# A block's last addition left to the next block or to the end, and a residual put ahead of a gate's step

## The chip, the cores and the metric

The kernel runs on one core of a Trainium2 chip. The metric is the time of one execution on the device in microseconds (us), as the median of a few runs. Beside it stands one profiled execution, which has its own time; the profile's span, from the first to the last instruction, is a little shorter than that time.

The engines: TensorE (PE; its weight loads are PEld), VectorE (DVE), ScalarE (ACT), GpSimd (POOL) and SyncE (SP, which here only issues DMAs). A "q" behind a name (POOLq) is the engine's sequencer: semaphore waits, branches, issuing.

## The reference, cut to what matters

```python
B, S, D = 4, 1024, 256            # T = B*S = 4096 tokens, 8 experts, hidden size 1024
x = x + ga * attention_like_scan(layernorm(x) * (1 + ca) + sa)      # y @ W_out, gated; "x1"
h = layernorm(x) * (1 + cb) + sb
scores = softmax(h @ Wg + bg);  top 2 experts per token, weights normed to 1
for e in range(8):
    y = gelu(h @ W1[e] + b1[e]) @ W2[e] + b2[e]
    output = output + y * combine_w[..., e]      # zero for experts that were not chosen
return x + gb * output
```

`ga`, `ca`, `sa`, `gb`, `cb` and `sb` come from a small product of the conditioning vector, one row per batch. All is float32.

## The kernel before, in words

**First part.** The 4096 tokens are cut into 8 chunks of 512. A chunk's projections, scan and output product run on all engines, interleaved with the second layernorm, the gate and the top-2 choice of earlier chunks. `o_pe` computes a chunk's output product into two PSUM tiles (`pya`), `o_resid` adds each to the residual `x` on VectorE (line 479) and stores the sum to `out`. `f_gate` computes the gate's logits on TensorE (line 540) and adds the bias on VectorE (line 547). The two PSUM slots of `pya` are those of `pye` below: the pool `ps_y` has two.

**Second part.** Each expert has a list of its tokens in DRAM. The lists are cut into blocks of 256 places; a block is two halves of 128. A table computed on the chip says which expert and which places block `j` has. Whole blocks come first, then blocks in which only the first half has tokens, then nothing. Up to 39 blocks are possible; 28 are surely whole, 32 surely exist. For block `j`:

- `fetch(j)`: `fetch_rows(j + 2)` loads the list entries (`ent`: a token's number and its weight; SyncE, line 788; four buffers in turn from block 8 on) and gathers the tokens' rows of `hx` into `hb` (GpSimd, line 801, one gather for each half, three buffers); `fetch_weights(j + 1)` loads `W1`, `b1`, `W2` and `b2` of its expert (SyncE, lines 819 to 822, two buffers, 2.1 MB per block).
- `b_up(j)`: the product with `W1` (line 859), gelu on ScalarE (line 868).
- `b_turn(j + 1)`: TensorE turns the next block's rows (line 843), VectorE copies them out of PSUM (`xT`, line 845).
- `b_down(j)`: for each half the product with `W2` (line 877, PSUM `pye`), then on VectorE the bias (line 885) and the weight and gate (line 886) into `yb`, which has four buffers, then on GpSimd one indirect DMA that adds the 128 rows to `out` (line 891). The DMA takes its row numbers from `ent`. Two blocks can share a token, so a block's additions wait until those of the block before have landed; the two halves of one block don't wait for each other.

**Order.** Every engine's order is the order in which the program is written (`manual_schedule`), so an engine that waits holds everything behind it. Waits are put in where an instruction reads or overwrites what another one, or a DMA, has yet to finish.

**Branches.** From block 28 on, `work_either` (line 1059) chooses between a whole and a half block; from block 32 on, `rest(j)` (line 1090) first asks whether block `j` exists, and the next block stands inside it. In each branch that skips DMAs of GpSimd, the queue of GpSimd increments the semaphores that they would have raised, in one instruction (INC_SWDGE_SEM in the profile), after waiting for what was raised before. In the branch for "no more blocks" this covers all eight such semaphores, and the increment waits for every DMA of GpSimd that is still under way. Behind the branches stands the end of the program: SyncE waits for all DMAs, each engine drains, and a barrier closes it (line 1125). With this input 36 blocks run: 0 to 30 are whole and 31 to 35 are half.

Of the kernel before, what the change touches and what calls it, by code (L numbers as in the profile page):

```python
# [9 lines left out]
F32 = mybir.dt.float32  # L10
I32 = mybir.dt.int32
AF = mybir.ActivationFunctionType
ALU = mybir.AluOpType
# [6 lines left out]
def tile_adaln_block(  # L20
# [32 lines left out]
    nc = tc.nc  # L53
    P = 128
    B, S, D = x.shape
    H = W_out.shape[0]
    E, _, F = W1.shape
    T = B * S
# [9 lines left out]
    HK = TK // P  # L68
# [16 lines left out]
    out_rows = out.rearrange("b s d -> (b s) d")  # L85

    const = ctx.enter_context(tc.tile_pool(name="const", bufs=1))
    apool = ctx.enter_context(tc.tile_pool(name="attn", bufs=1))
    deep = ctx.enter_context(tc.tile_pool(name="deep", bufs=2))
    work = ctx.enter_context(tc.tile_pool(name="work", bufs=3))  # L90
    small = ctx.enter_context(tc.tile_pool(name="small", bufs=2))
    xpool = ctx.enter_context(tc.tile_pool(name="blocks", bufs=2))
# [365 lines left out]
    def o_pe(c_):  # L458
        z, wo = X[c_]["z"], WO[c_ // NB]
        X[c_]["py"] = []  # L460
        for q in range(TPB // 2):
            py = ps_y.tile([P, 2, D], F32, tag="y", name=f"pya_{c_}_{q}")
            X[c_]["py"].append(py)
            for t in range(2):
                for hc in range(HC):
                    nc.tensor.matmul(  # L466
                        py[:, t, :],
                        lhsT=z[hc][:, ts(2 * q + t, P)],
                        rhs=wo[:, hc, :],
                        start=(hc == 0),  # L470
                        stop=(hc == HC - 1),
                    )

    def o_resid(c_):
        xb = X[c_]["x"]
        b, i = divmod(c_, NB)
        for q in range(TPB // 2):
            at = ds(2 * q, 2)
            nc.vector.tensor_add(xb[:, at, :], xb[:, at, :], X[c_]["py"][q])  # L479

        x1_stores.append(
            nc.sync.dma_start(
                out=out[b].rearrange("(n p) d -> p n d", p=P)[:, ts(i, TPB), :], in_=xb
            )
        )

    def f_stats(c_):
        X[c_]["stats"] = stats(X[c_]["x"], f"f{c_}")
# [43 lines left out]
    def f_gate(c_):  # L532
        b, i = divmod(c_, NB)
        if i == 0:
            R[b] = {"p": small.tile(sh, F32, tag="p", name=f"p_{b}")}
        hT = X[c_]["hT2"]
        pl = ps_tr.tile([P, TPB, E], F32, tag="tr", name=f"pl_{c_}")
        for n in range(TPB):
            for k in range(KC):
                nc.tensor.matmul(  # L540
                    pl[:, n, :],
                    lhsT=hT[:, k, ts(n, P)],
                    rhs=wg_sb[:, k, :],
                    start=(k == 0),
                    stop=(k == KC - 1),
                )
        nc.vector.tensor_add(
            R[b]["p"][:, ts(i, TPB), :], pl, bg_sb.unsqueeze(1).broadcast_to((P, TPB, E))
        )
# [221 lines left out]
    def seen(j: int):  # L771
        return EARLY_B * S if j < NE else T
# [18 lines left out]
    def fetch_rows(j: int):  # L791

        if j >= NJ:
            return
        if j >= NE:
            fetch_entries(j)
        hb = []
        for t in range(HK):
            g = turns(xpool, 3, [P, 2 * D], F32, f"hb{t}", j)
            BK[j]["gathers"].append(  # L800
                nc.gpsimd.indirect_dma_start(  # L801
                    out=g, out_offset=None, in_=hx[: seen(j), :],
                    in_offset=IndirectOffsetOnAxis(ap=BK[j]["ent"][:, t, 0:1], axis=0),
                    bounds_check=seen(j) - 1, oob_is_err=False,
                )
            )
            hb.append(g)
        BK[j]["hb"] = hb

    def fetch_weights(j: int):  # L810
        if j >= NJ:
            return
        wpool = pools["w"]
        e = entry(j, 0, E - 1)
        w1 = turns(wpool, 2, [P, KC, F], F32, "w1", j)
        w2 = turns(wpool, 2, [P, FC, D], F32, "w2", j)
        bb = turns(wpool, 2, [P, FC], F32, "bb", j)
        b2b = turns(wpool, 2, [P, D], F32, "b2b", j)
        nc.sync.dma_start(out=w1, in_=W1r[e])
        nc.sync.dma_start(out=bb, in_=b1d[e])  # L820
        nc.sync.dma_start(out=w2, in_=W2r[e])
        nc.sync.dma_start(out=b2b, in_=b2[ds(e, 1), :].broadcast_to((P, D)))
        BK.setdefault(j, {}).update(w1=w1, w2=w2, bb=bb, b2b=b2b)

    def fetch(j: int):

        fetch_rows(j + 2)
        fetch_weights(j + 1)
# [9 lines left out]
    def b_turn(j: int):  # L838
        hb = BK[j]["hb"]
        pt = ps_tr.tile([P, KC, TK], F32, tag="tr", name=f"ptx_{j}")  # L840
        for k in range(KC):
            for t in range(HK):
                nc.tensor.transpose(pt[:, k, ts(t, P)], hb[t][:, ts(k, P)], ident)  # L843
        xT = turns(xpool, 2, [P, KC, TK], F32, "xT", j)
        nc.vector.tensor_copy(xT, pt)  # L845
        BK[j]["xT"] = xT

    def b_up(j: int, half: bool = False):
        w1, bb, xT = (BK[j][n] for n in ("w1", "bb", "xT"))
        g = xpool.tile([P, FC, TK], F32, tag="g", name=f"g_{j}_{half}", bufs=1)  # L850
        BK[j]["g"] = g
        n = P if half else TK
        at_once = TB // n
        for f2 in range(FC // at_once):
            ph = ps_mm.tile([P, at_once, n], F32, tag="mm", name=f"ph_{j}_{f2}_{half}")
            for u in range(at_once):
                fc = at_once * f2 + u
                for k in range(KC):
                    nc.tensor.matmul(  # L859
                        ph[:, u, :],  # L860
                        lhsT=w1[:, k, ts(fc, P)],
                        rhs=xT[:, k, :n],
                        start=(k == 0),
                        stop=(k == KC - 1),
                    )
            for u in range(at_once):
                fc = at_once * f2 + u
                nc.scalar.activation(  # L868
                    g[:, fc, :n], ph[:, u, :], AF.Gelu_apprx_tanh, bias=bb[:, fc : fc + 1]
                )  # L870

    def b_down(j: int, half: bool = False, mid=None):
        g, w2, b2b, ent, hb = (BK[j][n] for n in ("g", "w2", "b2b", "ent", "hb"))
        for t in range(1 if half else HK):
            py = ps_y.tile([P, D], F32, tag="y", name=f"pye_{j}_{t}_{half}")
            for fc in range(FC):
                nc.tensor.matmul(  # L877
                    py,
                    lhsT=g[:, fc, ts(t, P)],
                    rhs=w2[:, fc, :],  # L880
                    start=(fc == 0),
                    stop=(fc == FC - 1),
                )
            yb = xpool.tile([P, D], F32, tag="yb", name=f"yb_{j}_{t}_{half}", bufs=4)
            nc.vector.tensor_add(yb, py, b2b)  # L885
            nc.vector.scalar_tensor_tensor(  # L886
                yb, yb, ent[:, t, 1:2].bitcast(F32), hb[t][:, D:], ALU.mult, ALU.mult
            )
            if t > 0:
                nc.gpsimd.memset(between, 0.0)  # L890
            ins = nc.gpsimd.indirect_dma_start(  # L891
                out=out_rows[: seen(j)],
                out_offset=IndirectOffsetOnAxis(ap=ent[:, t, 0:1], axis=0),
                in_=yb, in_offset=None, bounds_check=seen(j) - 1, oob_is_err=False,
                compute_op=ALU.add,
            )
            for other in BK[j]["acc"]:
                tc.declare_no_dep(ins.ins, other.ins, reason="a block's tokens are distinct")
            BK[j]["acc"].append(ins)
            if t == 0 and mid is not None:  # L900
                mid()
# [114 lines left out]
    last = NCH - 1  # L1016
# [4 lines left out]
    r_rank_pe(B - 2)  # L1021
    b_turn(1)
    o_pe(last)
    f_gate(last - 1)
    o_resid(last)
    f_stats(last)
    r_place(B - 2)
    drain(4)
# [20 lines left out]
    b_down(2)  # L1049
    tab["l"], ends_at = late_table()  # L1050

    def work(j: int, half: bool = False):
        b_up(j, half)
        if j + 1 < NJ:
            b_turn(j + 1)
        b_down(j, half)

    def work_either(j: int):
        with tc.If(n_whole > j) as whole:  # L1059
            work(j)  # L1060
        with whole.Else():
            work(j, True)


    sure_whole = (2 * T - E * P) // TK
    sure = 2 * T // TK
# [17 lines left out]
    )  # L1084
    for j in range(sure_whole, sure):
        fetch(j)
        work_either(j)

    def rest(j: int):
        with tc.If(n_blocks > j):  # L1090
            fetch(j)
            work_either(j)
            if j + 1 < NJ:
                rest(j + 1)

    rest(sure)
    order.close()


# [30 lines left out]
```

## Time and profile before

| | |
|---|---|
| median of 3 runs | 828.38 us (826.85 to 828.54) |
| profiled execution: its time, its span | 828.35 us, 826.6 us |
| TensorE busy | 802.2 us, 97% of the span |
| VectorE, ScalarE, GpSimd busy | 348.9, 250.7, 300.4 us |
| additions to `out` (line 891) | 62 of whole blocks, 5 of half blocks, 1.6 us each on GpSimd |
| one whole block, from addition to addition | 14.25 us |
| granted TensorE clock | 0.992 |

A row of the timeline has its start, its length, engine, line, operation and tiles, and in brackets how long the engine had been idle and what ended that. A row of a view of one line has the engine, the operation and the count, then the shortest, median and longest duration in ns, then the first and the last start in us. A row of the waits has who waited, for whom, the sum in us, the times and the longest. "DMA to landing" runs from the start of the DMA's row to the last of its data.

### The profile page before, as it was taken

To read this page: it belongs to the slowest core of one execution; us is meant where nothing else is said; L and a number is where in the kernel's file an instruction comes from. 1 tells how busy PE (TensorE), PEld (TensorE's weight loads), DVE (VectorE), ACT (ScalarE), POOL (GpSimd) and SP (SyncE) were. 2 spreads that over 40 slices of the span, in tenths; PEclk is the share of its full clock that TensorE was granted. 3 is DMA by queue.
4 is the path that set the end of the run, shared out by engine and by line. 5 is a ranking of instruction groups with operands and counts; after the bars stand their busy time and mean duration, and the time that the engine had idled before them with its cause. 6 is when DMAs were issued, how large, how long until landed. Compare 5 with 4: busy or idle time off the path is not lost. (4 is left out here: it accounts for less than half of the span.)

```text
span 826.6 us, 10561 instructions
## 1 busy us (share of the span) xinstructions
PE 802.2 (97%) x3447; PEld 606.4 (73%) x3447; DVE 348.9 (42%) x806; ACT 250.7 (30%) x577; POOL 300.4 (36%) x378
## 2 busy tenths in 40 slices
PE   6999999999999999999999999999999999999992
PEld 2454656564655658888888888888888888888982
DVE  4887776797688755544111112111111112121210
ACT  4434343535354253222222221312222221213220
POOL 2003010108203730778743433434342433334432
PEclk9999999999999999999999999999999999999997
DMA  8031221114101264698788677868777777777694
GB/s 307 1 112 44 85 91 66 52 45 78 45 27 33 78 199 146 149 248 195 196 245 236 182 217 207 233 198 219 218 205 223 197 208 208 225 197 194 194 287 125
DMA packets 110048, 132.57 MB, mean 160 GB/s; under 512 B 25686, under 2 KB 93978, under 8 KB 109984
## 3 DMA queue, kind: packets, MB, share of 16 engines
q1 hardware_dynamic: 86480, 101.76, 40.2%
q0 software_dynamic: 17776, 25.25, 13.7%
q10 hardware_dynamic: 5728, 4.77, 2.2%
q8 instruction: 33, 0.54, 0.3%
q14 instruction: 31, 0.25, 0.1%
HBM read 113.53 MB, written 21.75 MB: 164 GB/s over the span
## 5 line engine op out<-in xcount | busy, mean ns | idle before, releaser
L877 PE MATMUL pye_False<-w,g_False 128*128 128x256 f32 x992 | 221.1, 381 | 1.1 <-DVE x L479 1.1
L859 PE MATMUL ph_False<-xT,w 128*128 128x256 f32 x992 | 219.2, 379 | 0.0
L859 PEld LDWEIGHTS ph_False<-xT,w 128*128 128x128 f32 x992 | 188.3, 190 | 25.5
L877 PEld LDWEIGHTS pye_False<-w,g_False 128*128 128x128 f32 x992 | 187.2, 191 | 25.7 <-issue 1.1
L868 ACT ACTIVATE g_False<-ph_False,bb 128x256 f32<-128x256 f32 x248 | 104.0, 471 | 313.1 <-issue 225.3
L891 POOL DMA_INDIRECT out_dram<-yb_False,ent x46 | 73.8, 1604 | 188.7 <-DVE yb_False L886 188.7
L845 DVE COPY xT<-ptx 128x512 f32<-128x512 f32 x37 | 25.6, 691 | 198.9 <-PE ptx L843 198.9
L885 DVE TENSOR_TENSOR yb_False<-pye_False,b2b 128x256 f32<-128x256 f32 x62 | 26.3, 425 | 155.1 <-PE pye_False L877 152.6
L559 POOL DMA_INDIRECT lists<-pay,placei x64 | 68.2, 1066 | 12.6 <-issue 11.5
L801 POOL DMA_INDIRECT hb<-hx,ent x60 | 63.0, 1049 | 24.2 <-issue 16.5
L429 PE MATMUL pk<-hT,wk_sb 128*128 128x512 f32 x128 | 61.0, 599 | 0.8 <-ACT hT L405 0.8
L429 PE MATMUL pu<-hT,wu_sb 128*128 128x512 f32 x128 | 60.2, 592 | 0.0
L429 PE MATMUL pgi<-hT,wu_sb 128*128 128x512 f32 x128 | 60.1, 592 | 0.0
L429 PE MATMUL pgo<-hT,wu_sb 128*128 128x512 f32 x128 | 60.1, 592 | 0.0
L466 PE MATMUL pya<-wo,z 128*128 128x256 f32 x256 | 56.6, 379 | 0.0
L214 POOL TENSOR_TENSOR rstd_f<-rstd_f,expo 128x4 f32<-128x4 f32 x8 | 8.1, 1018 | 132.8 <-DVE rstd_f L213 132.8
L466 PEld LDWEIGHTS pya<-wo,z 128*128 128x128 f32 x256 | 48.6, 190 | 9.5 <-issue 3.3
L429 PEld LDWEIGHTS pgo<-hT,wu_sb 128*128 128x128 f32 x128 | 24.3, 190 | 30.6 <-issue 26.5
L429 PEld LDWEIGHTS pgi<-hT,wu_sb 128*128 128x128 f32 x128 | 24.3, 190 | 30.6 <-issue 30.6
L429 PEld LDWEIGHTS pu<-hT,wu_sb 128*128 128x128 f32 x128 | 23.7, 190 | 26.8 <-issue 24.4
L429 PEld LDWEIGHTS pk<-hT,wk_sb 128*128 128x128 f32 x128 | 23.1, 190 | 24.9 <-issue 20.5
L446 DVE TENSOR_TENSOR nu<-nu,pu 128x512 f32<-128x512 f32 x32 | 22.0, 686 | 45.4 <-PE pu L429 33.8
(188 smaller groups left out, 753.5 us busy)
## 6 DMA issues: line engine op xcount, KB each, us to landing
w<-in_L_ffn_W_dram SPq DMA_DIRECT2D x74, 1024.0 KB, 6.6
b2b<-in_L_ffn_b_dram SPq DMA_DIRECT2D x37, 128.0 KB, 6.8
hx<-gb ACTq DMA_DIRECT2D x4, 1024.0 KB, 6.1
out_dram<-x SPq DMA_DIRECT2D x8, 512.0 KB, 3.2
hx<-h SPq DMA_DIRECT2D x8, 512.0 KB, 3.0
x<-in_L_attn_x_dram SPq DMA_DIRECT2D x7, 512.0 KB, 6.0
wu_sb<-in_L_attn_W_ugg_dram SPq DMA_DIRECT2D x3, 512.0 KB, 5.5
mdf<-rows SPq DMA_DIRECT2D x3, 384.0 KB, 4.2
```

What stands on the lines that cost most here:

```text
L214: nc.gpsimd.tensor_tensor(rstd, rstd, expo[:, 0, :], ALU.pow)
L429: nc.tensor.matmul(ps, lhsT=w[:, k, col : col + P], rhs=hT[:, k, :], start=(k == 0), stop=(k == KC - 1),)
L446: nc.vector.tensor_mul(nu, nu, product(wu_sb, hc * P, "u"))
L466: nc.tensor.matmul(py[:, t, :], lhsT=z[hc][:, ts(2 * q + t, P)], rhs=wo[:, hc, :], start=(hc == 0), stop=(hc == HC - 1),)
L559: ins = nc.gpsimd.indirect_dma_start(out=lists[:, :], out_offset=IndirectOffsetOnAxis(ap=place, axis=0), in_=what, in_offset=None, bounds_ ...
L801: nc.gpsimd.indirect_dma_start(out=g, out_offset=None, in_=hx[: seen(j), :], in_offset=IndirectOffsetOnAxis(ap=BK[j]["ent"][:, t, 0:1], ax ...
L845: nc.vector.tensor_copy(xT, pt)
L859: nc.tensor.matmul(ph[:, u, :], lhsT=w1[:, k, ts(fc, P)], rhs=xT[:, k, :n], start=(k == 0), stop=(k == KC - 1),)
L868: nc.scalar.activation(g[:, fc, :n], ph[:, u, :], AF.Gelu_apprx_tanh, bias=bb[:, fc : fc + 1])
L877: nc.tensor.matmul(py, lhsT=g[:, fc, ts(t, P)], rhs=w2[:, fc, :], start=(fc == 0), stop=(fc == FC - 1),)
L885: nc.vector.tensor_add(yb, py, b2b)
L891: ins = nc.gpsimd.indirect_dma_start(out=out_rows[: seen(j)], out_offset=IndirectOffsetOnAxis(ap=ent[:, t, 0:1], axis=0), in_=yb, in_offse ...
```

## The change

It has two parts.

1. The additions of blocks from 31 on. In these blocks `b_down` writes the block's last half (in a half block: its only one) to a tile of its own, `last_y`, with one buffer, copies the row numbers to `last_at`, and issues no addition. The addition is issued at the start of the next block, inside `rest(j + 1)` ahead of `fetch(j + 1)`, or, for the last block that runs, behind all branches. The tile `yb` of the other halves has three buffers instead of four.
2. In front of block 0, `o_resid(last)` comes ahead of `f_gate(last - 1)` instead of behind it. TensorE's order is the same; on VectorE the two additions of line 479 now stand ahead of the addition of line 547, and SyncE's store of `x` moves with them.

```diff
+    last_y = xpool.tile([P, D], F32, tag="last_y", name="last_y", bufs=1)
+    last_at = const.tile([P, 1], I32, tag="last_at", name="last_at")
+
+    def add_rows(yb, at, n: int):
+        return nc.gpsimd.indirect_dma_start(
+            out=out_rows[:n],
+            out_offset=IndirectOffsetOnAxis(ap=at, axis=0),
+            in_=yb, in_offset=None, bounds_check=n - 1, oob_is_err=False,
+            compute_op=ALU.add,
+        )
+
-    def b_down(j: int, half: bool = False, mid=None):
+    def b_down(j: int, half: bool = False, mid=None, keep: bool = False):
...
-            yb = xpool.tile([P, D], F32, tag="yb", name=f"yb_{j}_{t}_{half}", bufs=4)
+            kept_back = keep and t == (0 if half else HK - 1)
+            if kept_back:
+                yb, at = last_y, last_at
+            else:
+                yb = xpool.tile([P, D], F32, tag="yb", name=f"yb_{j}_{t}_{half}", bufs=3)
+                at = ent[:, t, 0:1]
             nc.vector.tensor_add(yb, py, b2b)
             nc.vector.scalar_tensor_tensor(
                 yb, yb, ent[:, t, 1:2].bitcast(F32), hb[t][:, D:], ALU.mult, ALU.mult
             )
+            if kept_back:
+                nc.vector.tensor_copy(last_at, ent[:, t, 0:1])
+                continue
             if t > 0:
                 nc.gpsimd.memset(between, 0.0)
-            ins = nc.gpsimd.indirect_dma_start(
-                out=out_rows[: seen(j)],
...
+            ins = add_rows(yb, at, seen(j))
...
     o_pe(last)
+    o_resid(last)
     f_gate(last - 1)
-    o_resid(last)
     f_stats(last)
...
     for j in range(sure_whole, sure):
         fetch(j)
-        work_either(j)
+        work_either(j, j == sure - 1)
 
     def rest(j: int):
         with tc.If(n_blocks > j):
+            add_rows(last_y, last_at, T)
             fetch(j)
-            work_either(j)
+            work_either(j, True)
             if j + 1 < NJ:
                 rest(j + 1)
 
     rest(sure)
+    add_rows(last_y, last_at, T)
     order.close()
```

`work` and `work_either` hand the new argument `keep` on to `b_down`.

## The prediction

> **What bounds the kernel now.** First the page, for which engine is full:
>
> ```profile
> PE 802.2 (97%) x3447; PEld 606.4 (73%) x3447; DVE 348.9 (42%) x806; ACT 250.7 (30%) x577; POOL 300.4 (36%) x378
> PE   6999999999999999999999999999999999999992
> ```
>
> TensorE sets the time up to the last slices. So I ask for the waits of TensorE alone: the few that exist are the places where this change can win on it.
>
> ```profile
> PE pye_False L877 <- DVE x L479: 1.1, 1, 1.1
> PE ptx L843 <- DMA hb<-hx,ent: 1.0, 2, 0.8
> PE ph_True L859 <- DMA w<-in_L_ffn_W_dram: 0.2, 1, 0.2
> ```
>
> The first is the residual in front of block 0. The other two lie among the last five blocks, 31 to 35, which run the half branch (31 whole blocks give 62 additions; five rows carry "True"). Next the end, in the timeline:
>
> ```profile
> 810.20 1.00 POOL L801 DMA_INDIRECT hb<-hx,ent  x1 [0.31 <-issue]
> 811.57 0.42 DVE L885 TENSOR_TENSOR yb_True<-pye_True,b2b 128x256 f32<-128x256 f32 x1 [2.70 <-PE pye_True L877]
> 812.03 0.48 DVE L886 SCALAR_TENSOR_TENSOR yb_True<-yb_True,ent,hb 128x256 f32<-128x256 f32 x1
> 814.13 1.62 POOL L891 DMA_INDIRECT out_dram<-yb_True,ent  x1 [2.94 <-POOLq L1059]
> ```
>
> TensorE ends at 811.5, yet the span is 826.6: 15 us of tail. The views of the lines 1059, 1090, 1125 and (in the window of blocks 31 to 35) 891 say what fills it:
>
> ```profile
> L891 POOLq EVENT_SEMAPHORE  x5: 43/3837/4818, 778.7 to 809.5; - x5
> DMA to landing us min/median/max: 3.8/7.6/9.0
> L1059 POOLq INC_SWDGE_SEM  x5: 1376/1463/1583, 780.0 to 814.0; - x5
> L1090 POOLq INC_SWDGE_SEM  x1: 1608/1608/1608, 818.1 to 818.1; - x1
> L1125 POOLq DRAIN  x3: 46/107/5942, 819.9 to 826.4; - x3
> ```
>
> Addition 35 starts at 814.13 and lands 3.8 later (817.9). Only then does GpSimd's queue, in the branch for "no more blocks", run one increment of the skipped semaphores (1.6, from 818.1), then a drain of 5.9 (from 819.9), then the closing barrier (0.8). That is 12.5 us in series behind the start of the last addition. And SyncE, in the same window:
>
> ```profile
> SPq L788 <- DMA out_dram<-yb_True,ent: 10.5, 3, 5.0
> ```
>
> The lists of entries are held up three times until an earlier block's addition has landed, because the addition's offsets lie in the buffer to be refilled; the next weights are queued behind them.
>
> **What the skill says.** "Perfetto Trace Analysis", DMA Instruction — SWDGE (GPSIMD): a GpSimd DMA's row ends when its descriptors are written, not when data has moved. The trace agrees: row 1.61, landing 3.8 to 9.0. "DMA: Bandwidth & Descriptors", Anatomy of one DMA: some 2.0 us are fixed, mostly the write receipt; 3.8 - 1.6 = 2.2 here when little else moves. The same page, Queues, rings and completion order: each DMA engine alternates between queues that have work, which fits additions landing late while weights load. "VectorE: DVE Perf Modes", The DRAIN you can't avoid: boilerplate drains take about 12 ns on all engines; GpSimd's 5942 ns does not agree, so its cause is open and gets both bounds below.
>
> **The change part by part.**
>
> *The residual first.* VectorE now adds both halves of pya before the gate's logits. In before, the gate's TensorE work ends at 328.78 + 1.85 = 330.63 and the next product starts at 331.71, 1.08 late. The last pya ends at 328.94; one addition behind it (0.68) ends near 329.7, before 330.63. Gain 1.1 on TensorE. The gate's own addition (0.19) comes at about the same time, and nothing near waits for it. TensorE is full from here to 770, with 0 us of waits for weights, so the 1.1 reaches block 31.
>
> *Three buffers of yb instead of four.* A half's buffer now waits for the addition three before. In whole blocks (one per 14.25 us) that one was issued some 18 us or more earlier and lands within 9.5: nothing. Around blocks 1 to 4, where additions queue behind scatters, the tightest is block 4: its second half needs the addition of 387.93, landing 8.4 later (396.3), at 400.9. Nothing, with 4.5 to spare.
>
> *Additions of blocks 31 to 35 moved.* No DMA is added or dropped. GpSimd's order stays gathers(j+2), addition(j), gathers(j+3); what changes is that the increment of the half branch (1.4 to 1.6) and the branches stand before the addition, under a wait of 3.8 (median of the five), so they cost nothing until block 35.
>
> *Offsets in last_at.* One 128x1 copy per kept block; nearest row the 128x8 copy at 0.16. Entry buffers are free without a landing, so SyncE's 10.5 us of waits go, and weights may be asked for some 6 us earlier. TensorE's 1.2 us of waits on gathers and weights may shrink; I book nothing, since this only fills DMA gaps.
>
> *The new wait.* last_y has one buffer: VectorE's addition of block j+1 waits until kept addition j has landed. Behind it on VectorE stands the copy of xT for two blocks on, with several us of room; behind the next addition on GpSimd stand the gathers. Before, a landing was followed by the next start after 0.8 (780.12 + 7.6 = 787.7, next at 788.50); now by 0.42 + 0.48 + 0.16, 0.1 between them and 0.3 to start: 1.45. With the start of addition 31 at 780.12 - 1.1 + 0.1 = 779.1 and a landing time L, addition 34 starts at 779.1 + 3(L + 1.45). In before the five additions start at 780.12, 788.50, 795.69, 805.48 and 814.13, so 8.4, 7.2, 9.8 and 8.7 apart; less about 1 to notice the landing and start, four of them landed after some 6 to 9 us, against bursts of weights, and the last after 3.8, without. With the weights spread I take 7.0: 804.5 (before: 805.48).
>
> *The end.* After addition 34 GpSimd starts two gathers at +1.9 and +3.3 (as 445.04, 446.96, 448.33 in before, where nothing holds them up). The closing branch waits for their landing: 5.6 to 6.9 us in before, where transposes waited until 798.79 for gathers begun at 791.87 and 793.22; 4.5 assumed with the weights gone: 804.5 + 3.3 + 4.5 = 812.3. Then increment 1.6, wait and start 0.4: addition 35 starts at 814.3, by chance about as before. VectorE has finished last_y well before (804.5 + 7 + 1.15 = 812.7). So landing and increment (3.8 and 1.8 with their gaps) no longer stand ahead of the drain; behind the start remain descriptors 1.6, drain 5.9, barrier 0.9: 8.4 instead of 12.5. Span 814.3 + 8.4 = 822.7, gain 3.9. The 1.1 of TensorE is used up in the new wait.
>
> The profiled execution took 828.35, 1.75 more than its span, and the median is 828.38; so 822.7 + 1.75 = 824.45, forecast 824.4.
>
> *Bounds of the drain.* Before shows one, with everything landed. It may be a fixed cost from its start (taken), wait for the landing first (+2.2), or belong to the increment in front of it, and then vanish under the wait for the data: addition 35 then ends by landing, 3.8, plus about 1.3 for SyncE's last waits and the barrier: -3.3.
>
> **Rivals.**
> B, the drain starts to count at the landing: 824.4 + 2.2 = 826.6. For it: a drain means finishing work. Against: the page calls drains short.
> C, the drain belongs to the increment: 824.4 - 3.3 = 821.1. For it: it follows it at once.
> D, the chain of landings takes the gain: L = 7.6 as the median of before and gathers at 6: addition 34 at 806.2, gathers landed 815.5, addition 35 at 817.5, run 827.7; same.
> E, slower: place, the wait for last_y; price, 1.45 + L per block. With L = 9.0, the longest of before, addition 34 is at 810.4, gathers (6) landed at 819.7, addition 35 at 821.7, run 831.9. Before's time is reached with addition 35 at 818.2, that is L = 7.8; from L = 8.4 it is slower by over 0.2%. For it: three of the four landings were near or above that. Against: those coincide with bursts of 2 MB that SyncE released at the very landing.
> That the change doesn't do what it says is excluded: each engine runs its instructions in the order in which the program writes them.
>
> **How the numbers follow.** Forecast 0.48, B 0.16, C 0.10, D 0.14, E 0.12. No change is within 0.2%, 1.7 us, about what a measurement can tell. Faster: forecast and C whole, B for 0.13: 0.71. Same: D and the rest of B: 0.17. Slower: E, 0.12. The range leaves out most of E and the far side of C: 820.0 to 829.0; the faster cases alone: 820 to 826.7.
>
> **What would show it.** TensorE's wait on line 479 gone; SyncE's wait for yb_True gone, weights asked for earlier; VectorE waiting for landings before last_y; the large increment ahead of the last addition; a drain of about 6 directly behind that addition. Wrong if additions land in 8 us or more, if the last gathers land after 815, or if the drain grows.

## The result, and the profile after

The changed kernel takes 823.5 us (median of 6 runs, 822.57 to 824.49) against 827.96 us before (6 runs, 826.53 to 830.17): a ratio of 0.9955, 95% interval 0.9941 to 0.9970. By the ratio that is about 3.7 us faster (2.5 to 4.9), more than the 0.2% that the prediction took for what a measurement can tell. The forecast was 824.4 with a range of 820 to 829. A second set of executions of both kernels, below, gave a ratio of 0.9958 (0.9943 to 0.9973). The profiled execution took 824.49 us and its span is 822.8 us, 3.8 less than before; the prediction's sum had 822.7.

The total is near, but two of the terms behind it are not, and their errors partly cancel. So the profile after is read in three places: in front of block 0, in the last blocks, and at the end.

**In front of block 0.** First the timeline of TensorE of the kernel before, then that of the kernel after (start, length, engine, line, operation, tiles; in brackets the idle time before it and what ended it):

```profile
328.78 1.85 PE L540 MATMUL pl<-wg_sb,hT 128*128 128x8 f32 x16
331.71 8.83 PE L877 MATMUL pye_False<-w,g_False 128*128 128x256 f32 x32 [1.08 <-DVE x L479]
340.38 1.04 PE L403 MATMUL ptf<-ident,h 128*128 128x128 f32 x8
```

```profile
328.67 1.85 PE L540 MATMUL pl<-wg_sb,hT 128*128 128x8 f32 x16
330.38 7.15 PE L889 MATMUL pye_False<-w,g_False 128*128 128x256 f32 x32
...
338.10 0.77 PE L403 MATMUL ptf<-ident,h 128*128 128x128 f32 x5 [0.24 <-DVE h L241]
```

The idle time of 1.08 is gone. What the prediction had not seen stands in the second column: the same 32 products took 8.83 us before and take 7.15 now, 1.68 less. The table by stretch tells why; of before, then of after. A row has the stretch and its length, then the busy time and (with an x) the instructions begun of PE, PEld, DVE, ACT and POOL, then the granted TensorE clock, the busy share of the DMA engines and GB/s:

```profile
332.00:336.00 4.00, 4.00 (x12) 3.23 (x11) 3.76 (x20) 0.00 (x0) 1.74 (x3) 0.57 0.39 131
336.00:338.00 2.00, 2.00 (x11) 1.75 (x10) 1.81 (x6) 0.00 (x0) 1.79 (x4) 1.00 0.04 9
```

```profile
332.00:336.00 4.00, 4.00 (x20) 3.54 (x19) 3.61 (x19) 0.00 (x0) 2.86 (x5) 1.00 0.04 11
```

Directly behind the idle time TensorE ran at half clock for a while: a mean of 0.57 over 4 us, with 12 products begun where 20 begin now. At half clock for t us, t/2 is lost, and 1.68 lost makes t about 3.4. This profiled execution thus gained 1.1 + 1.7, gave about 0.4 back at the next waits (0.24 of it in the last row above), and its TensorE starts block 31 at 768.68 where before had 771.24, 2.6 ahead, 0.1 of it from an earlier start-up (the prediction had 1.1).

**In the last blocks.** Some of the waits of SyncE from 770 on, and of those of TensorE in the whole span, of the kernel after (who waited, for whom: us in all, times, longest):

```profile
...
SPq L788 <- DMA out_dram<-yb_False,ent: 5.7, 1, 5.7
SPq L821 <- PE ph_True L859: 4.7, 3, 3.5
SPq L822 <- DVE xT L845: 4.4, 1, 4.4
...
```

```profile
...
PE ptx L843 <- DMA hb<-hx,ent: 1.3, 1, 1.3
...
PE pye_True L889 <- ACT g_True L868: 0.6, 1, 0.6
PE ph_True L859 <- DMA w<-in_L_ffn_W_dram: 0.6, 1, 0.6
PE ptf L403 <- DVE h L241: 0.2, 1, 0.2
```

SyncE's 10.5 us of waits for the half blocks' additions are gone, as forecast (the 5.7 for a whole block's addition stood in before too, 5.2). But it now waits more for buffers of weights: 4.7 us at line 821, where before had 0.3 in the same blocks; the 4.4 at line 822 are not new (4.3). TensorE's waits in the half blocks went from 1.2 to 2.5 us, not down. The new wait is there too. Of the line of the additions, in the same window:

```profile
L876 POOL DMA_INDIRECT out_dram<-last_y,last_at x5: 1605/1612/1619, 777.6 to 814.0; - x5
...
  DVE last_y L902: 7.9, 2
...
DMA to landing us min/median/max: 3.8/6.3/7.5
```

The view puts two of VectorE's waits for `last_y` down to a landing, 7.9 us in all, but most of that time VectorE was waiting for TensorE's product as well. Line 902 starts at 784.08, 793.13 and 810.95 in blocks 32, 33 and 35, where the product had ended at 783.77, 792.29 and 809.99. So a landing held VectorE up three times, by 0.3, 0.8 and 1.0 us; in block 34 TensorE came last. The view's 6.3 is the middle of the three landings that it can tell. With the other two read from the starts of line 902 (0.19 us behind a landing where both are known), additions 31 to 34 landed after 6.3, 7.6, 7.5 and 7.0 us: the prediction's 7.0 was right.

**The end.** The timeline's last two lines, and the closing branch (1105) and the program's end (1143) by line:

```profile
811.81 0.15 DVE L907 COPY last_at<-ent 128x1 int32<-128x1 int32 x1
813.97 1.62 POOL L876 DMA_INDIRECT out_dram<-last_y,last_at  x1 [5.97 <-issue]
```

```profile
L1105 POOLq INC_SWDGE_SEM  x1: 1588/1588/1588, 811.1 to 811.1; - x1
```

```profile
L1143 POOLq DRAIN  x3: 46/113/8198, 813.7 to 822.5; - x3
```

The increment starts at 811.1, behind the closing branch's last wait (the sum had 812.3), and ends at 812.7. The last addition starts only 1.2 us behind that (the sum had 0.4), at 813.97 (forecast 814.3), and 2.0 us after the copy in the first line has its data ready. Its descriptors are written at 815.59, and the drain ends at 813.75 + 8.20 = 821.95. It is entered earlier than before, but ends 6.36 behind the descriptors: again some 6 us from the end of GpSimd's last work. From the start of the last addition to the end it is now 8.8 us, where before had 12.5 and the prediction 8.4.

### The profile page after: what moved, and what is told of

It reads as the page before. It is cut to its first block, busy times and chain, and to the rows that moved or that the text cites. A ratio compares the mean times of both kernels' runs of the same rounds, so it can differ in the third digit from the quotient of the medians.

```text
span 822.8 us, 10559 instructions
## 1 busy us (share of the span) xinstructions
PE 800.3 (97%) x3447; PEld 604.8 (74%) x3447; DVE 349.3 (42%) x811; ACT 250.7 (30%) x577; POOL 300.7 (37%) x378
## 4 chain that ended last, share of the span: by engine, by line
PE 83%; DMA 7%; DVE 4%; issue 3%; POOL 1%; ACT 1%; POOLq 0%; SPq 0%; another core or an unknown queue 0%; DVEq 0%
PE ph_False L859 24%; PE pye_False L889 23%; PE pya L466 7%; PE pk L429 6%; PE pu L429 6%; PE pgi L429 6%; PE pgo L429 6%; DMA out_dram<-yb_False,ent 3%; DMA out_dram<-last_y,last_at 2%; PE pl L540 2%; PE ptx L843 2%; DMA hb<-hx,ent 1%; PE ptf L403 1%; DMA ent<-lists 1%; PE pta L403 1%
## 5 line engine op out<-in xcount | busy, mean ns | idle before, releaser
L559 POOL DMA_INDIRECT lists<-pay,placei x64 | 68.2, 1066 | 12.5 <-issue 11.5
```

What stands on the lines that cost most here:

```text
L559: ins = nc.gpsimd.indirect_dma_start(out=lists[:, :], out_offset=IndirectOffsetOnAxis(ap=place, axis=0), in_=what, in_offset=None, bounds_ ...
```

## The experiments

### Each part alone

The first is the kernel before with only the residual moved:

```diff
     o_pe(last)
+    o_resid(last)
     f_gate(last - 1)
-    o_resid(last)
```

> The kernel before with the residual's additions ahead of the gate's step, and nothing else. Theory: block 0's down projection starts about 1.3 us earlier and the stretch at half clock (3.4 us at 0.5, from 332.0) is gone, so TensorE is about 2.6 us ahead at block 31, and the additions behind it move with it: about 828.0 - 2.6 = 825.4. Rival, the prediction's own sum: only the idle time of 1.1 goes, 826.9. Second rival: TensorE gains 2.6, but the additions of blocks 31 to 35 wait for one another's landing and take it back: within 0.5 us of before.

Measured: 825.04 us, ratio 0.9975 (0.9964 to 0.9987), 2.1 us under before (1.1 to 3.0). In its profile TensorE is 1.9 ahead behind block 0, no idle time and no half clock there, and it reaches the last down projection 2.9 ahead. Its last addition:

```profile
809.86 1.62 POOL L891 DMA_INDIRECT out_dram<-yb_True,ent  x1 [1.99 <-DVEq L1090]
```

In before that row starts at 814.13. The tail behind it is of the old kind (13.2 to the span's end). So nothing takes TensorE's gain back: the second rival falls. The interval doesn't choose between 1.1 and 2.6.

The second is the kernel after with the residual where it was, the reverse of that diff.

> The kernel after with the residual's additions behind the gate's step again, so with the kept additions alone. Theory, the parts add up: TensorE idles 1.1 us in front of block 0's down projection and then runs 3.4 us at half clock; the end keeps its shorter tail (about 8.8 us behind the start of the last addition) but everything in front of it is 2.6 later than in the kernel after: about 823.5 + 2.6 = 826.1, 1.9 under before. Rival, the prediction's sum: the end hangs on the chain of landings, which takes up what TensorE gains, so that the kept additions alone give 3.9: about 824.1.

Measured: 825.9 us, ratio 0.9985 (0.9976 to 0.9993), 1.2 us under before (0.6 to 2.0). Read by its sentence that the 1.1 of TensorE "is used up", the prediction gives 3.9 for the kept additions alone. Its sum says otherwise: it starts the chain of landings at 779.1, with the 1.1 already in it, and so gives 3.9 - 1.1 = 2.8. Both lie outside.

```profile
332.49 8.83 PE L889 MATMUL pye_False<-w,g_False 128*128 128x256 f32 x32 [1.08 <-DVE x L479]
...
815.40 1.62 POOL L876 DMA_INDIRECT out_dram<-last_y,last_at  x1 [4.77 <-issue]
```

The idle time of 1.08 and the half clock are back, and the end is that of the kernel after: the span ends 8.8 us behind the start of the last addition. The parts add to 0.40%; the two together gave 0.42 and 0.45%. With the residual moved as well, the kernel after is 0.27 to 0.30% faster than this one, give or take 0.17: TensorE's gain passes to the end.

### What the half clock follows

Is the half clock due to TensorE's low activity there, or to the place? The residual stays behind the gate's step, and products without use fill TensorE's idle time.

```diff
     f_gate(last - 1)
+    fill = ps_mm.tile([P, TK], F32, tag="mm", name="fill")
+    for _ in range(5):
+        nc.tensor.matmul(
+            fill, lhsT=BK[0]["w1"][:, 0, :P], rhs=BK[0]["xT"][:, 0, :], start=True, stop=True
+        )
     o_resid(last)
```

> The kernel before with five products of 128x256 without use (about 0.22 us each) between the gate's products and block 0's down projection, so that TensorE does not idle there, and the residual where it was. Theory, the half clock comes from the low activity (sixteen products of 8 columns, then 1.08 us idle): with the gap filled the down projection still starts at about 331.7 to 331.9, but the stretch at half clock is gone, and TensorE is 1.5 to 1.7 ahead behind it: about 826.4. Rival: the clock falls there for another reason (the load of that time), the stretch stays, and the time is that of before, 828.0 to 828.2.

Measured: 826.81 us, ratio 1.0001 (0.9988 to 1.0013): no gain to be seen. But the half clock is gone (the table by stretch has 1.00 from 328 to 340, and the 32 products took 7.07 us). The fill was too long: it ran as ten passes in 2.40 us, so that the down projection began 0.7 later than in before (1.0 later, counted from the start of the gate's products), and TensorE was only 1.0 ahead of before's profile behind it. A fill of two products fits:

> As the kernel with the gap filled, but with two products in place of five: each of them ran as two passes of 0.24, so that five took 2.40 and held the down projection up by 0.9 more than the gap of 1.08; two take 0.96 and fit it. Theory: the down projection starts where it does in before (331.7 with the same start-up), there is no stretch at half clock, TensorE is 1.7 ahead behind it, with the residual still behind the gate's step, and the time is 1.0 to 1.7 under before, about 0.998 to 0.9988. Rival, that the low clock belongs to the place or to the load: the stretch of 3.4 us stays and the time is that of before.

The timeline of TensorE in that run, and its table by stretch:

```profile
328.93 1.85 PE L540 MATMUL pl<-wg_sb,hT 128*128 128x8 f32 x16
330.63 1.11 PE L1027 MATMUL fill<-xT,w 128*128 128x256 f32 x4
331.70 7.15 PE L877 MATMUL pye_False<-w,g_False 128*128 128x256 f32 x32
```

```profile
332.00:336.00 4.00, 4.00 (x20) 3.54 (x19) 3.76 (x20) 0.00 (x0) 1.60 (x3) 1.00 0.39 135
```

The down projection starts at 331.70, as in before (331.71), with the residual still behind the gate's step, and yet takes 7.15 us: without the idle time there is no half clock, though the place is the same. The time is 826.06 us, ratio 0.9995 (0.9984 to 1.0005): 0.4 us under before, from 1.3 under to 0.4 over, at best the lower part of what was expected.

Why less than 1.7? The 81 timed executions of before in these three sets can be split by their mean granted clock: 50 at 0.992 or less (mean time 827.8) and 31 at 0.993 or more (826.2). A stretch of 3.4 us at half clock lowers the mean over the span by 0.002. With the gap filled, 27 of 28 executions are in the upper group, and with the residual moved 20 of 22. So the stretch may be missing in some 4 of 10 executions of before. By this estimate it costs 0.6 × 1.7 = 1.0 us on average, inside the short fill's interval, and with the idle time of 1.1 makes 2.1, what the residual alone gave. Two more profiles of before, unchanged, were taken to see:

> The kernel before, unchanged, for one more profile. Over 81 timed executions of it the mean granted clock lay at 0.989 to 0.992 in 50 (mean time 827.8) and at 0.993 to 0.995 in 31 (mean 826.2). Theory: the stretch of 3.4 us at half clock (which costs 1.7 us and lowers the mean clock of the span by 0.002) follows the idle time of 1.08 us in some executions and not in others; a profile with a mean clock of 0.990 to 0.992 has it, one with 0.994 or 0.995 has not, though the idle time is there in both. Rival: every execution has it, and the two groups come from the end of the span.

> The same once more: the stretch is there if the mean clock is 0.992 or less and absent if it is 0.994 or more (theory), or there in both cases (rival).

Of the first (829.04 us, mean clock 0.989), the timeline and the table by stretch:

```profile
331.51 10.20 PE L877 MATMUL pye_False<-w,g_False 128*128 128x256 f32 x32 [1.08 <-DVE x L479]
```

```profile
330.00:332.00 2.00, 0.92 (x5) 0.85 (x6) 1.53 (x4) 0.00 (x0) 0.00 (x0) 0.72 0.00 0
332.00:336.00 4.00, 4.00 (x11) 3.13 (x10) 3.65 (x20) 0.00 (x0) 1.94 (x3) 0.50 0.39 135
336.00:338.00 2.00, 2.00 (x7) 1.62 (x6) 1.93 (x5) 0.00 (x0) 1.62 (x5) 0.58 0.01 1
```

At the same idle time of 1.08 the low clock lasted twice as long here: 2 × 0.28 / 0.5 = 1.1 us up to 332, 4.0, and 2 × 0.42 / 0.5 = 1.7 behind 336, 6.8 in all. It began at 330.9, when TensorE had been idle for only 0.4 us (the gate's sixteen products end at 330.44). The second (827.9 us, clock 0.992) had the single stretch, with the products at 8.77 us. So its length varies, and all four profiles with that idle time (before three times, and the kept additions alone) show it, while none of the ten profiles without it shows one there. The length varies in steps. The traces' records of the clock have these stretches at 3.41 and 6.83 us, and the stretch at full clock in front of them is a whole number of times 3.413 us: 320.85 us in these four (94 times), 788.48 us (231 times) in the kernel with the split, further down.

The case that matters for the average, an execution of before at 0.994 without the stretch, wasn't caught in a profile: that it exists rests on the clocks alone. The rival, that the groups come from the end of the span, isn't excluded by these two profiles. The clock also halves at the end, from 2.1 to 5.3 us behind TensorE's last product, which by itself moves the mean by up to 0.002.

### The end

The last addition is issued inside the closing branch, ahead of the increment:

```diff
-        with tc.If(n_blocks > j):
+        with tc.If(n_blocks > j) as more:
             ...
                 rest(j + 1)
+            else:
+                add_rows(last_y, last_at, T)
+        with more.Else():
+            add_rows(last_y, last_at, T)
     rest(sure)
-    add_rows(last_y, last_at, T)
```

> The kernel after with the last addition issued in the closing branch itself, ahead of the increments of the skipped semaphores, not behind the branches. Theory: it no longer waits for the last gathers and starts at about 812.4 in place of 814.0, but its landing (3.8), the increment (1.6) and then the drain (about 6) and the barrier follow one after another as in before, 12.5 behind its start: span about 824.9, 2.1 over the kernel after, time about 825.6. Rival: the drain covers landing and increment (it counts from the last addition's descriptors), and then the span is 812.4 + 8.8 = 821.2, 1.6 under the kernel after.

Measured: 821.89 us, ratio 0.9935 (0.9916 to 0.9954), and a span of 821.5: as the rival had it (821.2), and my theory falls. Its timeline, then the closing branch and the program's end by line:

```profile
812.79 1.62 POOL L876 DMA_INDIRECT out_dram<-last_y,last_at  x1 [4.00 <-DVEq L1105]
```

```profile
L1105 POOLq INC_SWDGE_SEM  x1: 1633/1633/1633, 812.8 to 812.8; - x1
```

```profile
L1145 POOLq DRAIN  x3: 46/107/6042, 814.6 to 821.2; - x3
```

The increment runs beside the addition's descriptors (both from 812.8 for 1.6 us); a smaller one of 1.0 us had run at 807.9, while the last gathers were under way. It doesn't wait for this addition to land, as it had to in before, where the addition stood in the branch of its block and was one of the earlier ones that the closing branch waits for. The drain begins when both are done, 1.9 before the addition has landed (816.5), and takes the usual 6.

From the moment when VectorE has the last half ready to the end of the span, the profiles fall into three kinds: 12.9 to 14.2 us with the addition ahead of its landing and the increment (before three times, the residual alone, both fills), 10.3 to 11.5 with the increment ahead of the addition (the kernel after twice, the kept additions alone, and two kernels below), 9.0 here. By the times alone the step from 0.9955 to 0.9935 isn't clear, as the intervals overlap.

What does the drain wait for? The kernel after without the addition behind the branches, which leaves the last half of the last block out of the result:

```diff
     rest(sure)
-    add_rows(last_y, last_at, T)
```

> The kernel after without the addition behind the branches: the result lacks the last half of the last block. Theory: GpSimd's drain takes about 6 us from the end of its last work, whatever that is; with nothing behind the increment (which ends at about 812.7) it ends at about 818.8, so that the span is about 819.6. Rival, the drain waits for the landing of an addition in flight or belongs to the descriptors of one: with all landed it is short, well under 1 us, and the span ends by about 814 to 815.

One execution was measured; its span is 818.5, and of the program's end it shows:

```profile
L1142 POOLq DRAIN  x3: 46/107/5861, 811.8 to 818.2; - x3
```

The increment ended at 811.6 here. Every DMA of GpSimd had landed by 810.0, and the drain still took 5.86 us. So it waits neither for a landing nor for an addition's descriptors: it is a cost of about 6 us, behind the increment or the addition, whichever came last. What it does in that time stays open. It isn't there in every drain of GpSimd: the one at the program's start, behind a few memsets, took 0.17 us, and the two that follow at the end about 0.1 or less.

### What gates the last addition in the kernel after

Three kernels beside the kernel after on one chip:

> The kernel after once more, so that the next three stand beside it on one chip: 0.9955 of before, or 0.9960 if the parts of the first runs (0.9975 and 0.9985) add up and no more.

It gave 823.67 us, 0.9958 (0.9943 to 0.9973). In this profile (span 820.9) the kept additions start at 778.02, 786.38, 794.56 and 803.04, and the last at 812.18. Here no wait for `last_y` is put down to a landing, but two of them were ended by one:

```profile
778.02 1.61 POOL L876 DMA_INDIRECT out_dram<-last_y,last_at  x1 [3.21 <-DMA ent<-lists]
785.09 0.42 DVE L902 TENSOR_TENSOR last_y<-pye_True,b2b 128x256 f32<-128x256 f32 x1 [3.59 <-PE ph_True L859]
```

The product that the view names belongs to the next block; block 32's own had ended at 784.16, and addition 31 landed 6.9 us behind its start, at 784.90. In block 34 it is the same (line 902 at 801.75, the product done at 800.69, the landing at 801.56). In blocks 33 and 35 TensorE came last. So the two are near balance, and which one ends last changes from block to block and from execution to execution.

The last addition itself starts 2.6 us after its data are ready here (2.0 in the first profile), and 0.3 in the kernel with the addition in the branch. What holds it up in the kernel after is the increment and what follows that, behind the closing branch's last wait.

```diff
+            if j == 36:
+                fetch_rows(37)
-            fetch(j)
+            if j == 35:
+                fetch_weights(36)
+            else:
+                fetch(j)
```

> The kernel after without the gathers for block 37 (this input has no such block; they are moved into the branch of block 36, so nothing of the result is left out). Theory: the closing branch waits for addition 34 to land as well as for these gathers (the last semaphores it waits for came at 810.79 and 811.09), so that without them addition 35 starts only about 0.3 earlier: 0.3 under the kernel after. The prediction's view, that the landing of these gathers alone gates the last addition: addition 35 at about 812.4, as early as VectorE has its data, 1.6 under the kernel after.

Measured: 822.94 us, 0.9943 (0.9929 to 0.9958), within the spread of the kernel after. In its profile the increment still begins only at 809.87, right behind the landing of addition 34 (809.76), and the last addition starts at 812.66. So the gathers alone do not gate it. Whether dropping them is worth 0.3 or 1.6 us was not settled.

```diff
-            if kept_back:
-                yb, at = last_y, last_at
+            to = last_y if kept_back else yb
             nc.vector.tensor_add(yb, py, b2b)
             nc.vector.scalar_tensor_tensor(
-                yb, yb, ...
+                to, yb, ...
```

> The kernel after, but with the bias added into a rotating buffer, so that only the scaling (0.48) and the copy of the offsets (0.16), and not the addition of the bias (0.42), wait for the landing of the kept addition before. Theory, the chain of landings sets the starts of additions 33 to 35: each step is 0.4 to 0.5 shorter, addition 34 starts about 0.5 to 0.9 earlier and so does the end: 0.5 to 0.9 under the kernel after. Rival, the down projections of TensorE set these starts: no difference.

Measured: 824.04 us, 0.9952 (0.9939 to 0.9965): no difference to be seen, but the 0.5 to 0.9 us that were expected are smaller than what these intervals can tell, so neither theory nor rival falls. VectorE waited 2.3 us for landings alone. In this profile (span 825.1) TensorE waited 2.04 us for a gather at 799.4, and its clock fell behind that idle time too:

```profile
799.00:802.00 3.00, 2.59 (x8) 2.23 (x9) 0.69 (x1) 0.00 (x0) 1.00 (x1) 0.56 1.13 330
802.00:806.00 4.00, 4.00 (x24) 3.56 (x23) 0.89 (x3) 0.00 (x0) 0.00 (x0) 0.90 0.60 220
```

A wait of 1.3 at transposes in the kernel after (its single longest in the half blocks) brought no such drop.

The fourth takes the addition in the branch, the split and the dropped gathers together:

> The last addition in the closing branch, the bias added into a rotating buffer and no gathers for block 37, together. Theory: in the kernel with the addition in the branch addition 35 started at 812.79, 1.4 behind the landing of addition 34; with the bias out of the chain it starts 0.4 to 0.9 earlier, the tail stays at 8.7, and the time is 0.4 to 0.9 below that kernel's, about 0.9927 of before. Rival: TensorE's last down projection sets it, and it stays at 0.9935.

Measured: 821.1 us, 0.9922 (0.9909 to 0.9935), the best here: 6.5 us under before, and 0.36% (about 0.2 either way) under the kernel after on the same chip. Its last addition starts at 810.66, and the span ends 8.6 later. Against the addition in the branch alone (0.9935) the intervals overlap, so what the other two edits add is not shown.

## Why the prediction was right, and where it was not

**The residual: the wait right, the size not.** Of the step "Gain 1.1 on TensorE" the idle time is gone as forecast. The term was mis-sized because I priced a wait by its length alone: the residual alone gives 2.1 us (1.1 to 3.0). In the profile shown of before, 3.4 us at half clock followed the wait, 1.7 us more. A word of warning was to be had: the Trainium skill, "TensorE: Matmul & The Clock Gate", Part 1, says that a monitor sets the array's clock by how busy it has lately been, and that an idle window brings half of it; the windows are about 3.4 us long and run freely. The runs agree in the length (3.41 and 6.83 us, and steps of 3.413) and in its varying from execution to execution. Its table "Why this matters for your kernels" asks only for no idle gaps over about 3 us; here 1.08 us was enough, directly behind 1.85 us of sixteen products of eight columns. That those products count as low activity is my reading. The repeated profile of before supports it, as the clock fell there after 0.4 us of idle time behind them, where waits of 1.3 to 1.5 in the half blocks brought no drop; but no run took them away. And the mean clock, 0.992, stood in the table of before: I had not asked where the missing 0.008 lay (0.002 in this stretch, the rest at the idle end).

**"The 1.1 of TensorE is used up in the new wait": wrong.** This step failed, and it doesn't fit the prediction's own sum, which carries the 1.1 along. The residual gives 2.1 us alone, and on top of the kept additions about as much (2.2 to 2.5, give or take 1.4). The chain of landings is there, and its steps are as forecast (8.7 us a block in the kernel after, 8.3 in its repeat, 8.45 forecast). But it begins with addition 31, which starts as soon as TensorE's product allows, and after that a landing that comes last does so 0.3 to 1.5 us behind TensorE's product. So an earlier TensorE makes the whole chain earlier.

**The end: the start and the tail right, the comparison not.** Addition 35 came at 813.97 (814.3), partly by luck: the closing branch's wait ended 1.2 earlier than in the sum, and the addition followed the increment 0.8 later. The tail is 8.8 (8.4: the drain ends 6.36, not 5.9, behind the descriptors). But I set 814.3, with the residual moved, against before's 814.13, without, and so took the shorter tail for nearly all gain. That comparison mixes the parts: with only the residual moved, the last addition starts at 809.86, and with only the additions kept, at 815.40. Keeping them back thus delays the last one by 0.7 to 4.1 us in these profiles, since it now waits for the last gathers, for addition 34 and for an increment of 1.6, before it saves about 4 behind. What is left is 1.2 us (0.6 to 2.0), where the sum had 2.8.

So the forecast of 824.4 was near 823.5 by luck: a term too small (1.1 for about 2.1) met one too large (2.8 for about 1.2). The range held because both errors were small beside it.

**SyncE and the transfers: right.** Its waits for additions went and nothing was won by it. TensorE's waits in the last blocks are 1.1 to 3.4 us in the profiles with kept additions and 0.5 to 2.7 in those without: no gain, as booked. In the kernel after, SyncE asked for the weights of block 34 7.0 us earlier (781.84 for 788.88) and then waited for weight buffers to come free (line 821).

**Three buffers of yb, offsets in last_at: right.** No wait on either; the copy takes 0.15 us.

**The drain and the rivals.** Of the three bounds, the one taken holds nearly: a fixed cost, but from the end of GpSimd's work and not from the drain's own start (813.75, ahead of the addition). B (counts from the landing) falls by both later runs: with the addition in the branch it ended 4.2 behind the landing, and without any addition it still took 5.86. C (belongs to the increment) falls, since the drain of the kernel after has the addition between it and the increment. D and E, the chain with landings of 7.6 or 9 us, did not come: the four landings that the chain waits for took 7.1 us on average in the kernel after, 7.6 at most.

## What to carry to other kernels

A short idle time of TensorE is not priced by its length alone: look at the granted clock in the microseconds around it, and where a mean clock is under 1, ask in which stretches. When two edits meet at one end, compare each against the kernel without it, not against the start time that happens to stand in the old profile. Where a profile names who ended a wait, hold the name against the times: here a product of the next block stood for a landing. And look for steps at the end that can run side by side: with the addition and the increment so, the span ended 8.9 to 9.0 us after the last data were ready, against 10.3 to 11.5 and 12.9 to 14.2 in the two orders.

## What was not expected of the hardware

- TensorE fell to half clock at 1.08 us of idle time, for 3.41 us in three profiles and for 6.83 in one; behind waits of 1.3 to 1.5 in the half blocks it did not, behind one of 2.04 it did.
- The stretches at half clock (but for the one that a trace's end cuts off) and the full clock in front of them are whole multiples of 3.413 us in these traces: 320.85 us is 94 of them, 788.48 us 231.
- GpSimd's first drain at the program's end took 5.86 to 6.04 us where the increment was among its last work, and ended 6.2 to 6.4 behind an addition's descriptors where those came last; data in flight did not lengthen it.
- Incrementing the skipped semaphores takes 1.0 to 1.6 us of GpSimd's queue, but runs beside the writing of an addition's descriptors.
